# Pairs of tiles only, with queries, keys and values made three units ahead and passed through DRAM

## The chip, the cores and the metric

The kernel runs on one core of a Trainium2 chip, in fp32 throughout. The metric is the device time of one execution in microseconds; the median of three runs counts. The engines are named as in the profile: PE is TensorE (PEld its weight load), DVE is VectorE, ACT is ScalarE, POOL is GpSimd, and SP is the engine whose queue issues nearly all DMAs.

## The reference

Eight images (B = 8) of 512 tokens (S) with 576 features (D) pass through a rotation in a 64-dimensional subspace that depends on a condition, and then through one transformer block whose shifts, scales and gates depend on the same condition. The block has 16 heads of 36 features (H, DH), and its attention is unusual: it runs over the 16 heads *of one token*, not over tokens, so each token has a 16 x 16 matrix of scores.

```python
U, _ = qr(P)                                   # 576 x 64
R = expm(skew(silu(cond) @ W.T + b))           # one 64 x 64 per image
z = einsum('btn,nd->btd', x, U)
x = x + einsum('btd,nd->btn', einsum('btd,bde->bte', z, R) - z, U)
shift_a, scale_a, gate_a, shift_m, scale_m, gate_m = split(silu(c) @ ada_w + ada_b, 6)
h = modulate(layernorm(x), shift_a, scale_a)
q, k, v = (h @ qkv_w + qkv_b).reshape(n, t, 3, H, DH)
attn = softmax(einsum('nthd,ntkd->nthk', q * DH**-0.5, k))
o = einsum('nthk,ntkd->nthd', attn, v).transpose(0, 2, 1, 3).reshape(n, t, d)
x = x + gate_a * (o @ proj_w + proj_b)
h = modulate(layernorm(x), shift_m, scale_m)
x = x + gate_m * (gelu(h @ fc1_w + fc1_b) @ fc2_w + fc2_b)     # hidden width 2304
```

The transpose ahead of the last reshape mixes heads and tokens: row blocks of the projection's input hold many tokens of one head. In each image the 128 rows of one *tile* of the projection come from 8 x 16 places of the attention result. So the attention result goes to DRAM and is read back in the other order.

## The kernel before

A prologue (QR of P, the skew matrices and their exponentials, the modulation) takes some 230 us. Then the work is cut into tiles of 128 tokens, four per image, and these pieces, each a function below, are strung together by hand:

- `rotation(b)` gives six pieces: two of `project_z` (z of half an image, from a transposed copy of x) and four of `rotate` (PE adds the rotation to a tile, VectorE sums it with x, the result is stored to DRAM as `xr` and normalised: `normed`, L130). `feature_major(b, half)` turns the normalised tiles on PE and ScalarE modulates them into `hT`.
- `qkv(b, i)` gives four groups for tile i: ten matrix instructions each (five chunks of D, two passes in the profile's count) into 432 columns of PSUM, and a copy by ScalarE (L803) into a tile `qkv` in SBUF, of which there are three buffers.
- `attention(b, ts)` works on the tiles named in `ts` on VectorE: for each tile four products (L821) and four reductions (L827) of 2304 elements per partition give the scores; then one softmax over all tiles of `ts`, its exponential on ScalarE (L834); then four products and four reductions per tile with the values (L843, L849). The result is stored to DRAM by SP.
- `Projection` loads that result in projection order (`at`) and the rotated x. `turn(t)` transposes a tile (L882) and ScalarE copies it to `aT` (L883); `product(t, n)` multiplies half of the columns (L893), and VectorE gates and adds (L895, L896); `norm(t)` normalises; `turn_normed(cs)` transposes the normalised rows (L911) for the mlp.
- `mlp` runs fc1 (L938) and fc2 for a pair of tiles in nine steps, with weights streamed from DRAM by SP. fc2 takes seven products instead of eight for a pair (sums of blocks: POOL makes those of the activations, L1029 to L1032, and `next_sums`, called nine times early in the kernel, makes those of the weights and stores them as `comb_d`). `mlp_plain` is the ordinary product for a unit of one tile. `aside` slips pieces of the next image's rotation and its `feature_major` between the steps of an mlp.

A *unit* is what one projection and one mlp work on. There are seventeen: the first two tiles of image 0 are units of one tile each, all others are pairs. The main loop takes a unit k, and around its projection places the qkv groups of unit k + 1: three groups ahead of `turn(0)`, one between `turn(0)` and `product(0, 0)`, three ahead of `turn_normed((0, 1))`, one after it. The attention of unit k + 1 is written after the mlp of unit k.

The text gives each engine its instructions in written order only where `manual_schedule` says so: in the kernel before, for POOL until unit 2. Elsewhere a scheduler orders each engine's instructions when the program is built, by priority (earlier written first) and by its estimate of when operands are ready. PE, ScalarE, POOL, VectorE and SP each run their own list in order and wait for each other by semaphores. Buffers in SBUF and banks in PSUM are rings: `ps_mm`, which qkv, rotation and projection share, has two banks, so the third product in a row waits until the first has been read.

## Time and profile before

| | |
|---|---|
| Median of three runs | 2204.76 us (2204.02 to 2207.38) |
| The profiled execution | 2202.1 us, its span 2200.2 us, mean granted clock of TensorE 0.958 |
| Busy: PE, PEld | 2085.2 us (95%), 1562.6 us (71%) |
| Busy: DVE, ACT, POOL | 1795.9 us (82%), 390.0 us (18%), 703.2 us (32%) |
| Moved by DMA | 355.55 MB, mean 162 GB/s; SP's queue holds 16 engines for 54.6% of the span |
| VectorE's longest waits | 134.6 us for the end of an mlp (L1075), 119.8 us for ScalarE's copy of qkv (L821) |

The page first gives the busy time of each engine, then the span in forty slices of 55 us with one digit per slice (9 is 90% or more), among them the clock that TensorE was granted. A line of a group gives the line of the kernel, the engine, output and inputs by their names in the program, shape, count, busy time and mean duration. In a timeline a row is a run of equal instructions: start, duration, engine, line, and in brackets how long the engine was idle just before, with the one that released it. A row of windows gives a stretch: its length, then busy time and count for PE, PEld, DVE, ACT and POOL, the granted clock, the busy share of the sixteen DMA engines and the GB/s that they moved. Rows of DMAs give count, size and the median time from issue to landing.

### The profile page before, as it was taken

What the parts mean: (1) busy time and instruction counts of PE and PEld (TensorE: products, weight loads), DVE (VectorE), ACT (ScalarE), POOL (GpSimd) and SP (SyncE); (2) the same over time, 40 slices, a digit from 0 to 9 for tenths busy, and PEclk for the clock granted to TensorE, in tenths of its full rate; (3) what the DMA queues carried; (4) which work ended last, traced back from release to release, by engine and by line L of the source; (5) the groups of instructions that cost most, each with busy time, mean ns of one, the idle gap of its engine ahead of it and who ended that gap; (6) DMA issues with size and microseconds to landing.
All of it is one profiled execution on the core that took longest, in us unless ns stands there. A gap on an engine that the chain in (4) does not pass through costs nothing.

```text
span 2200.2 us, 26294 instructions
## 1 busy us (share of the span) xinstructions
PE 2085.2 (95%) x9609; PEld 1562.6 (71%) x9609; DVE 1795.9 (82%) x2450; ACT 390.0 (18%) x831; POOL 703.2 (32%) x882
## 2 busy tenths in 40 slices
PE   6896797899999999999999999999999999999998
PEld 3475455667777777868686868777776868686877
DVE  8997498799986979888896979697978889797930
ACT  2232121121021212111111112111211112111110
POOL 2341033113333233424241424243332324142422
PEclk9955698999999999999999999999999999999999
DMA  8201145864757374837384656656573737374764
GB/s 277 86 2 71 45 117 171 285 214 136 218 168 202 118 211 123 234 97 215 113 248 127 170 158 196 162 152 181 158 227 97 221 107 214 106 215 113 210 177 123
DMA packets 214291, 355.55 MB, mean 162 GB/s; under 512 B 82670, under 2 KB 101563, under 8 KB 214164
## 3 DMA queue, kind: packets, MB, share of 16 engines
q1 hardware_dynamic: 214164, 353.88, 54.6%
q8 instruction: 77, 1.26, 0.2%
q14 instruction: 50, 0.41, 0.1%
HBM read 321.43 MB, written 32.39 MB: 161 GB/s over the span
## 4 chain that ended last, share of the span: by engine, by line
PE 57%; DVE 19%; issue 13%; DMA 5%; POOL 3%; ACT 1%; SPq 1%; POOLq 0%; DVEq 0%; ACTq 0%
PE fc L938 24%; PE fc L1044 7%; PE fc L1049 5%; PE qkvp L796 5%; DVE sc L827 4%; DVE pv L843 3%; DVE att L849 3%; PE fc L1046 2%; PE p L1059 2%; DVE qk L821 2%; DMA out<-x 2%; PE zps L731 2%; DMA w<-in_fc_w 1%; PE fc L1001 1%; PE rot L739 1%
## 5 line engine op out<-in xcount | busy, mean ns | idle before, releaser
L938 PE MATMUL fc<-h2T,w 128*128 128x256 f32 (+3 forms) x3060 | 659.9, 369 | 11.4 <-DMA w<-in_fc_w 10.0
L938 PEld LDWEIGHTS fc<-h2T,w 128*128 128x128 f32 (+1 forms) x3060 | 551.9, 192 | 86.1 <-issue 9.8
L796 PE MATMUL qkvp<-wqkv,hT 128*128 128x432 f32 (+1 forms) x1280 | 478.6, 527 | 2.8 <-ACT hT L775 1.4
L821 DVE TENSOR_TENSOR qk<-qkv 128x2304 f32<-128x2304 f32 x128 | 328.9, 2570 | 122.4 <-ACT qkv L803 119.8
L796 PEld LDWEIGHTS qkvp<-wqkv,hT 128*128 128x128 f32 (+1 forms) x1280 | 239.6, 190 | 205.6 <-issue 195.4
L843 DVE TENSOR_TENSOR pv<-sc,qkv 128x2304 f32<-128x2304 f32 x128 | 331.4, 2589 | 3.2
L849 DVE TENSOR_REDUCE att<-pv 128x144 f32<-128x2304 f32 x128 | 326.5, 2551 | 3.2
L827 DVE TENSOR_REDUCE sc<-qk 128x64 f32<-128x2304 f32 x128 | 326.3, 2549 | 2.9
L1029 POOL TENSOR_TENSOR ss<-gt 128x128 f32<-128x128 f32 x135 | 143.4, 1062 | 578.3 <-ACT gt L946 578.3
L946 ACT ACTIVATE gt<-fc 128x512 f32<-128x512 f32 (+1 forms) x153 | 87.5, 572 | 728.7 <-PE fc L938 728.5
L803 ACT COPY qkv<-qkvp 128x432 f32<-128x432 f32 x128 | 66.5, 519 | 542.7 <-PE qkvp L796 542.5
L1049 PEld LDWEIGHTS fc<-wt,ss 128*128 128x128 f32 x1080 | 150.5, 190 | 14.2
L1049 PE MATMUL fc<-wt,ss 128*128 128x144 f32 x1080 | 154.4, 286 | 0.0
L1044 PE MATMUL fc<-wq,gt 128*128 128x288 f32 x540 | 153.0, 405 | 0.0
L140 POOL TENSOR_TENSOR rstd_m<-rstd_m,mhalf 128x1 f32<-128x1 f32 x32 | 19.9, 622 | 371.3 <-DVE rstd_m L139 366.0
L1075 DVE TENSOR_TENSOR u<-u,fc 128x288 f32<-128x288 f32 x15 | 6.8, 454 | 134.6 <-ACT u L1074 134.6
L1044 PEld LDWEIGHTS fc<-wq,gt 128*128 128x128 f32 x540 | 100.8, 189 | 21.3
L893 PE MATMUL pj<-w2q_p,aT 128*128 128x288 f32 x384 | 105.5, 411 | 3.0 <-ACT aT L883 1.4
L954 POOL TENSOR_TENSOR x<-x,mt 128x288 f32<-128x288 f32 x64 | 53.1, 831 | 172.3 <-DVE mt L953 172.3
L1031 POOL TENSOR_TENSOR ss<-gt,ss 128x128 f32<-128x128 f32 x135 | 99.8, 740 | 10.6
L1032 POOL TENSOR_TENSOR s<-gt 128x128 f32<-128x128 f32 x135 | 93.1, 690 | 0.0
L893 PEld LDWEIGHTS pj<-w2q_p,aT 128*128 128x128 f32 x384 | 70.0, 189 | 29.8 <-issue 6.2
(255 smaller groups left out, 2344.4 us busy)
## 6 DMA issues: line engine op xcount, KB each, us to landing
w<-in_fc_w SPq DMA_DIRECT2D x306, 320.0 KB, 3.5
wq<-in_fc_q SPq DMA_DIRECT2D x135, 432.0 KB, 3.4
wt<-comb_d SPq DMA_DIRECT2D x135, 432.0 KB, 4.5
w2q_p<-in_proj_w SPq DMA_DIRECT2D x34, 432.0 KB, 4.9
w<-in_fc_w SPq DMA_DIRECT2D x36, 288.0 KB, 4.6
xT<-in_x_t SPq DMA_DIRECT2D x16, 640.0 KB
w2t_p<-in_proj_w SPq DMA_DIRECT2D x34, 288.0 KB, 4.8
xt<-in_x SPq DMA_DIRECT2D x32, 288.0 KB, 4.5
```

Source lines behind the costliest of these rows:

```text
L796: nc.tensor.matmul(ps, lhsT=hT[0:k, c, i * 128 : (i + 1) * 128], rhs=wqkv[0:k, c, n * N : (n + 1) * N], start=c == 0, stop=c == NK - 1,)
L821: nc.vector.tensor_tensor(pr, q[:, c * HC : (c + 1) * HC].unsqueeze(2).to_broadcast([128, HC, H, DH]), k.unsqueeze(1).to_broadcast([128, H ...
L827: nc.vector.tensor_reduce(sc2[:, t, c * HC : (c + 1) * HC, :], pr, AX.X, ALU.add)
L843: nc.vector.tensor_tensor(pr, sc2[:, t, c * HC : (c + 1) * HC, :].unsqueeze(2).to_broadcast([128, HC, DH, H]), v.unsqueeze(1).to_broadcast ...
L849: nc.vector.tensor_reduce(att[:, c * HC : (c + 1) * HC, :], pr, AX.X, ALU.add)
L893: nc.tensor.matmul(ps, lhsT=aT[0:k, c, :], rhs=w, start=c == 0, stop=c == NK - 1)
L938: nc.tensor.matmul(ps[:, k], lhsT=w1[0:n, c, :], rhs=h2T[0:n, c, 0 : NU * 128], start=c == 0, stop=c == NK - 1,)
L1029: nc.gpsimd.tensor_tensor(ss[:, 0], gt[:, 0, 1], gt[:, 1, 1], ALU.add)
L1031: nc.gpsimd.tensor_tensor(ss[:, 2], gt[:, 1, 0], ss[:, 1], ALU.subtract)
L1032: nc.gpsimd.tensor_tensor(s3s[g], gt[:, 0, 0], gt[:, 0, 1], ALU.subtract)
L1044: nc.tensor.matmul(p[k], lhsT=whole[k][0], rhs=whole[k][1], start=g == 0, stop=stop)
L1049: nc.tensor.matmul(bank[:, side], lhsT=lhs, rhs=rhs[:, n * QUARTER : (n + 1) * QUARTER], start=False, stop=stop, skip_group_check=True,)
```

## The change

All units are pairs, sixteen of them, and `mlp_plain` is gone. A qkv tile is made in six groups of 288 columns. Each group is copied by ScalarE to a small buffer `qs` (two of them) and stored to DRAM (`tok_d`) by a DMA that ScalarE issues; `attention` loads the tile back through SP. Only the first two tiles of image 0 stay in SBUF. The groups are made three units ahead: image 0's four tiles and image 1's four tiles before the first projection, then two tiles in each of units 1 to 10, one tile in each of units 11 to 14, none in unit 15. Rotation and `feature_major` run two images ahead (in the first unit of each image) rather than one.

`attention` becomes a generator of which `ops(n, att)` takes n VectorE operations; its softmax is taken per tile rather than per unit, and the first tile's shares are worked out after the second tile's scores. Up to the norm of the first unit, all of the order is written by hand, for VectorE as for POOL. In the projection of a unit, all groups but the last six come ahead of `turn(0)`, none stands between `turn(0)` and `product(0, 0)`, five come ahead of `turn_normed((0, 1))` and one after it. The bias row of fc2 is no longer kept as a constant (`b2`) but loaded for each image into `gb2`.

```diff
 def qkv(b, i):
-        tok = tiles.tile([128, 3 * D], F32, tag="qkv", name=f"qkv_{b}_{i}", bufs=3)
-        N = 3 * D // 4
+        stay = b == 0 and i < 2
+        if stay:
+            tok = toks[b, i] = tiles.tile([128, 3 * D], F32, tag="qkv", name=f"qkv_{b}_{i}", bufs=3)
...
-            nc.scalar.copy(tok[:, n * N : (n + 1) * N], ps)
-        toks[b, i] = tok
-        return [lambda n=n: group(n) for n in range(4)]
+            if stay:
+                nc.scalar.copy(tok[:, cols], ps)
+            else:
+                qs = tiles.tile([128, HALF], F32, tag="qs", name=f"qs_{b}_{i}_{n}")
+                nc.scalar.copy(qs, ps)
+                nc.scalar.dma_start(out=tok_d[b][i * 128 : (i + 1) * 128, cols], in_=qs)
+        return [lambda n=n: group(n) for n in range(6)]
 def attention(b, ts):
-        own = [toks.pop((b, i)) for i in ts]
+        for i in ts:
+            if (b, i) not in toks:
+                toks[b, i] = tiles.tile([128, 3 * D], F32, tag="qkv", name=f"qkv_{b}_{i}", bufs=3)
+                nc.sync.dma_start(out=toks[b, i], in_=tok_d[b][i * 128 : (i + 1) * 128])
+            own.append(toks.pop((b, i)))
...
+        yield from scores(0)
+        raised(0)
+        yield from scores(1)
+        raised(1)
+        shares(0)
+        yield from values(0)
+        shares(1)
+        yield from values(1)
 
-    units = [(0, (0,)), (0, (1,)), (0, (2, 3))] + [(b, (i, i + 1)) for b in range(1, B) for i in (0, 2)]
+    units = [(b, (i, i + 1)) for b in range(B) for i in (0, 2)]
...
+    held.enter_context(tc.manual_schedule(engines={mybir.EngineType.Pool, mybir.EngineType.DVE}))
+    first[0]()
     feature_major(0, 0)
+    q = qkv(0, 0)
+    now(q[:2])
+    first[2]()
+    now(q[2:4])
+    first[3]()
+    next_sums()
+    now(q[4:])
+    q = qkv(0, 1)
+    att = attention(*units[0])
+    ops(4, att)
+    first[4]()
+    next_sums()
     feature_major(0, 0)
+    ops(2, att)
+    first[5]()
+    now(q)
     next_sums()
     feature_major(0, 1)
+    now(qkv(0, 2))
+    ops(4, att)
     next_sums()
+    second[0]()
+    ops(4, att)
+    second[1]()
     next_sums()
+    ops(2, att)
+    second[2]()
+    now(qkv(0, 3))
+    second[3]()
+    ops(2, att)
+    next_sums()
+    second[4]()
+    ops(2, att)
+    second[5]()
+    next_sums()
+    feature_major(1, 0)
+    now(qkv(1, 0))
+    ops(4, att)
+    next_sums()
+    now(qkv(1, 1))
+    feature_major(1, 1)
+    now(qkv(1, 2))
+    q = qkv(1, 3)
+    now(q[:3])
+    ops(4, att)
+    next_sums()
+    ops(40, att)
+    next_sums()
+    att = attention(*units[1])
+    ops(6, att)
+    ahead = {0: q[3:]}
+    tiles_of = [(unit[0], i) for unit in units[4:] for i in unit[1]]
+    for k in range(1, N - 1):
+        for tile_ in [tiles_of.pop(0) for _ in range(2 if k < 11 else 1)]:
+            ahead.setdefault(k, []).append(tile_)
     for k, (b, ts) in enumerate(units):
         if ts[0] == 0:
             gate_a, gate_m = gate_rows(0, b), gate_rows(1, b)
             gb2 = big.tile([128, D], F32, tag="gb2", name=f"gb2_{b}")
-            nc.gpsimd.tensor_tensor(gb2, gate_m, b2, ALU.mult)
+            nc.sync.dma_start(out=gb2, in_=fc2_b.to_broadcast([128, D]))
+            nc.gpsimd.tensor_tensor(gb2, gb2, gate_m, ALU.mult)
...
+        now(q[:front])
+        pr.turn(0)
+        pr.product(0, 0)
+        pr.turn(1)
+        pr.product(0, 1)
+        pr.norm(0, gb2)
+        pr.product(1, 0)
+        pr.product(1, 1)
+        pr.norm(1, gb2)
         if k == 0:
+            ops(1, att)
+        now(q[front : max(front, len(q) - 1)])
+        pr.turn_normed((0, 1))
+        now(q[max(front, len(q) - 1) :])
         pr.turn_normed((2, 3))
         pr.turn_normed((4,))
+        if k == 0:
+            held.close()
         aside = {}
+        if ts[0] == 0 and b + 2 < B:
+            p = rotation(b + 2)
+            aside = {1: p[0], 2: p[1], 4: p[4], 5: p[5]}
+            aside[3] = lambda two=p[2:4]: now(two)
+            aside |= {7: lambda: feature_major(b + 2, 0), 8: lambda: feature_major(b + 2, 1)}
+        mlp(pr, gate_m, aside)
+        ops(40, att)
+        if k + 2 < N:
+            att = attention(*units[k + 2])
```

## The prediction, made before the changed kernel ran

> **What bounds the kernel now.** I read the page's busy row and slices first, to see which engine is full and where it is not; then the chain's shares; then the timelines of PE (TensorE) where the slices have holes; then windows for clock and DMA.
>
> ```profile
> PE 2085.2 (95%) x9609; PEld 1562.6 (71%) x9609; DVE 1795.9 (82%) x2450; ACT 390.0 (18%) x831; POOL 703.2 (32%) x882
> PE   6896797899999999999999999999999999999998
> DVE  8997498799986979888896979697978889797930
> PEclk9955698999999999999999999999999999999999
> PE 57%; DVE 19%; issue 13%; DMA 5%; POOL 3%; ACT 1%; SPq 1%; POOLq 0%; DVEq 0%; ACTq 0%
> ```
>
> A slice is 55 us. From the tenth on PE is full: what runs there costs its PE time, and only less PE work or fewer holes shorten it. Slices 3 to 8 (110 to 495 us) have holes and a low granted clock. The change begins at about 240 us, so I looked at PE from there to the first pair's mlp.
>
> ```profile
> 268.82 1.33 PE L771 MATMUL htr<-ident,xm 128*128 128x128 f32 x5 [10.92 <-DVE xm L141]
> 279.88 14.78 PE L796 MATMUL qkvp<-wqkv,hT 128*128 128x432 f32 x40 [0.33 <-DVE xt L747]
> 343.06 1.09 PE L911 MATMUL h2tr<-ident,xm 128*128 128x128 f32 x4 [6.30 <-DVE xm L141]
> 361.75 4.58 PE L938 MATMUL fc<-h2T,w 128*128 128x128 f32 x20 [7.96 <-DMA w<-in_fc_w]
> 519.67 2.65 PE L938 MATMUL fc<-h2T,w 128*128 128x256 f32 x11
> ...
> 225.00:245.00 20.00, 18.37 (x56) 12.31 (x56) 4.49 (x14) 4.61 (x15) 1.64 (x13) 0.54 0.28 93
> 365.00:385.00 20.00, 18.52 (x121) 16.43 (x120) 10.51 (x6) 1.67 (x5) 0.00 (x0) 0.97 0.99 275
> sum 300.00, PE 257.90 PEld 174.95 DVE 247.13 ACT 55.99 POOL 68.90; mean PE 17.19 PEld 11.66 DVE 16.48 ACT 3.73 POOL 4.59
> ```
>
> The brackets are the wait before a row and its releaser. Between 225 and 525 us PE is idle 42 us, and partly at half clock besides: VectorE is late twice, and a single-tile mlp waits 8 us for weights while the DMA engines stand at 0.99. Counting every gap over the pace at which matmuls follow each other in full stretches (363 ns for 432 columns, 243 for 288), I find 80 us lost between 225 and 520 us, and under 1 us per unit later.
>
> **A check of the method.** At 519.67 before still owes 15 pair mlps (69.56 us each at pace), 14 pair projections (11.90), 26 qkv tiles (14.51), 6 rotations of an image (11.36): 1655.5 us. 519.7 + 1655.5 = 2175.2; its last matmul ends at 2192.4. So 17.2 us are stalls (8 in the last unit), and 7.8 us of tail make the span. The sum is good to a few us, and the front is where the change can win.
>
> **The change, part by part.**
>
> *Pairs only.* Two single units (43.1 us each) become one pair unit (81.5): 4.7 us less PE work, and the weights are streamed 16 times rather than 17, so the stretch at DMA share 0.99 with its waits (8.0 us, and 4.3 us in fc2) goes.
>
> *qkv in six groups.* A tile is 40 matmuls of 363 ns before, 60 of 243 after: 14.51 against 14.56 us, 1.6 us over 32 tiles. With the rest of the re-cutting PE work after 225 us falls by 3 us only. All else is stalls.
>
> *The front, written by hand.* Queries, keys and values of eight tiles and image 1's rotation now come before the first projection. I followed the written order from the rows above with before's durations: VectorE's attention operation every 2.59 us, a rotated tile 3.1 us, copies 0.4.
> - VectorE's first score at 253.5, as before (image 0's rotation of tiles 2 and 3 keeps its place around it). PE waits for VectorE to free a bank behind the rotations: tile 1 of qkv starts at 273.5 (279.9 before), ends 290.1.
> - VectorE holds behind a rotation that PE has behind qkv of tile 2 (302 to 312), and again (332 to 341). PE waits in turn for VectorE 314 to 321.5 and 343 to 350.5. These are new stalls of the written order; before's scheduler could run attention in between.
> - Image 1's rotation brings two xT and four xt loads and four xr stores onto SP, in windows of DMA share 0.3 to 0.4: no wait. The nine next_sums (POOL, 5.6 us each beside a busy VectorE) put their comb_d stores on SP too; the last three hold SP until 358, 363 and 369, and the store of the first attention tile, behind them, goes at 373: its re-load lands at 384, just in time.
> - qkv of image 1: 353.6 to 384; attention of unit 0 is done at 387, its re-load through DRAM (store 6.9, load 4.2 us by the page) at 398; PE has qkv to do until 410; projection to 420; first fc1 at **429.8**.
>
> The clock: the three PE pauses are 5.6, 7.8 and 7.5 us.
>
> ```profile
> 268.00:272.00 4.00, 1.79 (x6) 1.40 (x7) 3.78 (x3) 1.84 (x5) 0.15 (x1) 0.50 0.27 74
> 272.00:276.00 4.00, 4.00 (x10) 2.73 (x9) 3.96 (x2) 0.00 (x0) 0.00 (x0) 0.50 0.00 0
> 279.00:283.00 4.00, 3.67 (x12) 1.83 (x11) 3.48 (x13) 0.26 (x1) 0.69 (x2) 1.00 0.67 226
> ```
>
> After the 10.92 us pause the granted clock (column after POOL) is 0.50 for two windows with 5.8 us of PE work: 2.9 us lost. The Trainium skill ("TensorE: Matmul & The Clock Gate", "What's actually happening") says that a pause of about 3.4 us halves the clock until some 3.4 us of sustained work: 1.7 us lost. It speaks against a written order that makes three such pauses: 5 us by the page, 9 by the row. I took 2 each, as the shorter pause at 361.75 gives nearly that; the difference is 3 us of the range.
>
> *After 429.8* are owed 16 mlps (1113.0), 15 projections (178.5), 24 qkv tiles (349.4), 6 rotations (68.2), less 1.0 done early: 1708.1. 429.8 + 1708.1 = 2137.9, against 2175.2.
>
> *Steady units lose cover.* In before a group of qkv stands between the turn of the attention result and its product:
>
> ```profile
> 1058.59 0.71 PE L882 MATMUL atr<-ident,at 128*128 128x128 f32 x5
> 1059.14 3.79 PE L796 MATMUL qkvp<-wqkv,hT 128*128 128x432 f32 x10
> 1062.77 1.62 PE L893 MATMUL pj<-w2q_p,aT 128*128 128x288 f32 x6
> ```
>
> After, the product comes at once and waits for ScalarE's copy of aT; unit 0 of before, which had no cover either, waited 0.56, plus the lost pace: 0.73 us, x15 = 11. Before turn_normed five groups (12.1 us) replace three (10.9); xm was late by 0.46 us here, so 0 to 0.6 a unit remain. I take 17 us for 15 units, 8 for the last, 7.8 tail: 2137.9 + 32.8 = **2170.7** span.
>
> *The way through DRAM.* 30 tiles x 0.885 MB, out and back: 53 MB more, some 11 MB less for the dropped unit, on 355.55: about a tenth of the engines' time. Windows of a unit with rotation:
>
> ```profile
> 1080.00:1090.00 10.00, 9.54 (x34) 5.05 (x33) 9.97 (x6) 2.99 (x7) 4.20 (x2) 1.00 0.00 0
> 1120.00:1130.00 10.00, 10.00 (x49) 8.48 (x48) 10.00 (x11) 1.19 (x2) 2.86 (x7) 1.00 0.90 295
> 1140.00:1150.00 10.00, 9.99 (x53) 8.27 (x52) 9.93 (x7) 3.20 (x6) 5.74 (x6) 1.00 1.00 226
> w<-in_fc_w SPq DMA_DIRECT2D x306, 320.0 KB, 3.5
> ```
>
> The stores fall in qkv stretches (share 0.00 to 0.5, last but two columns aside), which have room; the loads come in the mlp, at 0.9 to 1.0, yet no matmul waits there today. The skill ("DMA: Bandwidth & Descriptors", "Issuing engines are not separate DMA queues") says that stores issued from ScalarE run on the same 16 engines as SP's loads and only spare issue time: so they are no free lane. A unit's 3.5 MB at the 295 GB/s seen is 12 us of full engines; the page would let all 12 hurt in a full stretch, the row lets nothing. Bounds: 0 and 12 us per unit; I take 0, since prefetch is a buffer deep everywhere and the mean share is 0.55, and keep 3 us per unit for the range. Below nothing: weights are no longer starved early, already counted.
>
> On SP the loads of a tile wait for its stores and for VectorE to free one of three qkv buffers; behind them stand weights (one every 5 us). The stores land three units earlier, so only VectorE's pace can hold them: 0 to 3 us per unit, taken 0. On ScalarE the qs buffers (two) are free when a store has landed, 3.0 us for xr of twice the size, against 4.85 us of PE between uses of one: hidden, with 1.8 us to spare. gb2's load, its product on POOL and per-tile softmax (some 15 more exps, each with table loads of 1283 ns to and fro) lie beside an 18% busy ScalarE; gelu can come 2 to 3 us late against 4 to 6 us slack: 0, bound 0.7 a unit, what one such slip cost before (L1046 on POOL). VectorE has about 97 us a unit, 107 with a rotation, against PE's 110 and 122; in the last five units PE's 96: bound 0 to 5 us in all.
>
> **Sum.** The profiled execution took 2202.1 us (span 2200.2); the median 2204.76 is 4.6 above the span. 2170.7 + 4.6 = 2175.
>
> **Rivals.**
> - *Slower: SP's queue holds the weights.* A qkv load waiting for VectorE's buffer delays every fc1 and fc2 load behind it; tolerance is one prefetch, about 3.7 us. From 2.3 us lost a unit (34 over 15 units) the gain is gone; at 4 us: 2175 + 60 = 2235. For: shares of 1.00 in the mlp, one queue for all loads, and VectorE 82% busy. Against: VectorE waited 134.6 us for the mlp's end and 119.8 us for qkv, so it has slack. 0.2.
> - *The front is worse.* Each engine waits for the other in written order; if PE's first mlp starts 20 us later, at 450: 2195; at 30: no change. For: five alternating waits of 5 to 10 us. 0.18, a third of it at no change.
> - *Front or steady state better.* Schedules without the 17 us, or a first fc1 at 420: 2157. 0.15.
> - The forecast: 0.47.
>
> **Numbers.** Faster than 2200.3 (0.2% is 4.4 us, about what can be told from no change): 0.47 + 0.15 + 0.11 = 0.73; within: 0.06; slower: 0.21. The range 2155 to 2213 leaves out the far ends of the first and third rival.
>
> **What would show it.** Right: PE's first fc1 of 256 columns near 430, the same 115 us a unit after it, a wait of pj for aT of 0.5 us in each unit, no DMA row under PE's waits in the mlp. Wrong: "fc <- DMA w" or "wt" as large waits in steady units (first rival); htr, rot or qkvp waiting for VectorE by tens of us before 430 (second); VectorE's waits for qkv gone but PE waiting for xm or att instead.

## The result, and the profile after

The changed kernel takes 2266.4 us (median of four runs, 2263.4 to 2267.3) against 2206.1 us for the kernel before, run beside it on the same chip: a ratio of 1.0267, 95% interval 1.0246 to 1.0289. The forecast was 2175, with a range of 2155 to 2213. The kernel is slower by 60 us, and outside the range. The profiled execution has a span of 2265.3 us, 94.6 above the 2170.7 of the sum.

The page of the changed kernel: busy times, the slices of VectorE, the queue of the new stores, and the chain of waits by engine.

```profile
PE 2107.7 (93%) x10087; PEld 1689.8 (75%) x10087; DVE 1820.3 (80%) x2530; ACT 427.2 (19%) x916; POOL 683.9 (30%) x918
DVE  8897668599999999999999997986979536832940
q10 hardware_dynamic: 25920, 26.55, 3.7%
DVE 42%; PE 37%; issue 10%; POOL 4%; DMA 4%; ACT 1%; SPq 0%; ACTq 0%; POOLq 0%; DVEq 0%
```

VectorE's total is hardly changed (1820 against 1796 us), but its slices are. Before, 7s and 8s alternated with 9s to the end. Now sixteen slices in a row (nine to twenty-four, 450 to 1360 us) are at 9, and later ones fall to 5, 3 and 2. In the chain VectorE has 42% and PE 37%, where PE had 57% and VectorE 19%. The average hides this: VectorE is full in the first half, and in the second it has less and less to do.

To place the loss I cut the span at the first transpose of a unit's attention result (`atr`, the start of its projection). The column of forecast is the prediction's own sum, cut at the same places (work of 808.2 and 723.9 us in the two middle rows, plus the 17 us of stalls).

| us | forecast | after | difference |
|---|---|---|---|
| start to unit 1's `atr` | 524.3 | 543.3 | +19 |
| unit 1's to unit 8's (units 1 to 7) | 816 | 859.4 | +43 |
| unit 8's to unit 15's (units 8 to 14) | 733 | 760.0 | +27 |
| unit 15's to the end | 97.3 | 102.7 | +5 |

Windows over units: length, then busy time and count of PE, PEld, DVE, ACT and POOL, granted clock, DMA share and GB/s. First the kernel before: six units in its middle, and of these one with a rotation and one without.

```profile
590.25:1293.93 703.68, 700.33 (x3066) 533.34 (x3064) 584.26 (x504) 120.82 (x221) 243.76 (x283) 1.00 0.59 171
...
823.24:947.21 123.97, 123.49 (x543) 93.71 (x542) 103.31 (x97) 23.48 (x44) 44.31 (x49) 1.00 0.60 178
947.21:1058.59 111.38, 110.91 (x483) 84.58 (x482) 95.37 (x69) 16.96 (x30) 37.31 (x44) 1.00 0.56 158
```

And the changed kernel: units 1 to 7, units 8 to 14, and then unit 3 (without rotation), unit 4 (with one) and a stretch of the length of a late unit.

```profile
543.25:1402.66 859.41, 827.01 (x3835) 677.25 (x3834) 840.31 (x678) 166.72 (x307) 269.68 (x323) 0.99 0.64 193
1402.66:2162.61 759.95, 738.31 (x3476) 610.65 (x3474) 527.79 (x476) 132.73 (x246) 239.65 (x316) 0.99 0.64 195
...
789.55:905.93 116.38, 113.13 (x523) 93.36 (x522) 114.72 (x84) 21.79 (x38) 38.73 (x44) 0.99 0.69 194
905.93:1039.03 133.10, 127.88 (x584) 103.62 (x582) 130.37 (x117) 28.40 (x53) 38.37 (x50) 0.97 0.64 197
1796.00:1894.00 98.00, 96.94 (x462) 81.10 (x462) 37.05 (x45) 14.59 (x28) 28.87 (x45) 1.00 0.62 195
```

Before, VectorE worked 95 us in a unit without rotation and 103 in one with, and PE stood 3.4 us in all six. After, it works 115 and 130 us, where PE's work is 110.6 and 121.9: VectorE sets the pace. In units 1 to 7 it works 840 of 859 us, in the late stretch 37 of 98.

Its groups in units 1 to 7 (count, then busy time and mean ns) say what it works on:

```profile
L859 DVE TENSOR_TENSOR pv<-sc,qkv 128x2304 f32<-128x2304 f32 x72 | 189.5, 2632 | 1.1
L866 DVE TENSOR_REDUCE att<-pv 128x144 f32<-128x2304 f32 x72 | 183.1, 2543 | 1.1
L831 DVE TENSOR_TENSOR qk<-qkv 128x2304 f32<-128x2304 f32 x68 | 177.1, 2604 | 0.8
L838 DVE TENSOR_REDUCE sc<-qk 128x64 f32<-128x2304 f32 x68 | 173.0, 2544 | 0.9
```

That is 280 large operations in seven units, 40 each. A unit's attention is 2 tiles of 16 large operations, 32; before held that number in every unit. In the changed program the list of VectorE has, between the ends of the mlps of successive units, 40, 41, 40, 41, 40, 41, 40 of them, and then 33, 32, 32, 8, 24, 8, 24 and 0. The order is fixed when the program is built. In the text `ops(40, att)` stands behind each mlp and takes the 32 of one unit; that the scheduler moves some of the next unit's forward, because in its estimate data three units ahead are always ready, is my reading and was not traced in the scheduler. What the trace shows is that the brake of before is gone. In the six middle units of before VectorE waited 48 us for qkv; in units 1 to 7 of the changed kernel the same products waited 0.8 us (row L831 above).

```profile
L821 DVE TENSOR_TENSOR qk<-qkv 128x2304 f32<-128x2304 f32 x44 | 112.2, 2551 | 48.8 <-ACT qkv L803 48.0
```

Seventeen extra operations of 2.6 us in two units are 44 us, and the two rows above have 245.1 against before's 198.7.

What this does to PE: the projection of unit 4, on PE and on VectorE (start, duration, and in brackets the wait and its releaser).

```profile
907.56 1.72 PE L921 MATMUL pj<-w2q_p,aT 128*128 128x288 f32 x6 [0.92 <-ACT aT L911]
...
912.10 1.14 PE L921 MATMUL pj<-w2t_p,aT 128*128 128x288 f32 x4
...
915.61 2.36 PE L921 MATMUL pj<-w2q_p,aT 128*128 128x288 f32 x6 [2.37 <-DVE pt L923]
917.76 2.13 PE L921 MATMUL pj<-w2t_p,aT 128*128 128x288 f32 x4
```

```profile
909.95 2.55 DVE L838 TENSOR_REDUCE sc<-qk 128x64 f32<-128x2304 f32 x1
912.53 2.56 DVE L831 TENSOR_TENSOR qk<-qkv 128x2304 f32<-128x2304 f32 x1
915.01 0.45 DVE L923 TENSOR_TENSOR pt<-pj,gate 128x288 f32<-128x288 f32 x1
```

The third product needs a bank that `pt` must read first. `pt` takes 0.45 us, but two attention operations stand ahead of it in VectorE's list, so PE waits 2.37 us. The wait costs more than its length: the four matmuls of the last row take 2.13 us where the same four took 1.14, and the granted clock of that stretch is 0.52.

```profile
917.00:920.00 3.00, 3.00 (x8) 2.13 (x7) 2.39 (x6) 0.00 (x0) 0.00 (x0) 0.52 0.94 308
```

In units 1 to 7 the clock stood at half four times, for 3.4 us each, three of them at a wait for `pt` like this one. That is some 7 of the 43 us. In fs3_lead, the last experiment below, it did not fall in these units.

Four of PE's waits in the whole kernel, in total, times and longest:

```profile
PE pj L921 <- DVE pt L923: 17.6, 11, 3.5
PE qkvp L797 <- DVE xt L746: 12.4, 2, 8.1
PE pj L921 <- ACT aT L911: 9.9, 13, 0.9
PE qkvp L797 <- ACT qs L808: 7.2, 3, 4.4
```

These rows are smaller than the 94.6 us: much of the loss is stretched matmul rows (the busy PE of 827 us in units 1 to 7 has 808 us of work; the halved clock is a part of that) and short gaps. That is why the windows, not the list of waits, carry the reading.

Running ahead has an end: by unit 8 VectorE has used up the lead of three units. Its 353rd large operation, the first for unit 11, needs the tile that unit 8 has only just made. The last of its six stores is issued at 1403.29, SP's load of the tile waits for the stores, and VectorE for the load:

```profile
1403.29 0.33 ACTq L809 DMA_DIRECT2D tok<-qs  x1
1406.64 0.33 SPq L822 DMA_DIRECT2D qkv<-tok  x1
1412.89 2.56 DVE L831 TENSOR_TENSOR qk<-qkv 128x2304 f32<-128x2304 f32 x1 [4.36 <-DMA qkv<-tok]
1415.37 0.82 DVE L923 TENSOR_TENSOR pt<-pj,gate 128x288 f32<-128x288 f32 x2
```

VectorE is idle 4.36 us for a tile's load, for an attention operation that nobody needs for three units yet, while `pt` stands behind it; PE waits 3.48 us for that `pt`. From here the list can only keep up with the tiles as they are made: 32 operations in units 8 to 10, which make two tiles each, and 8 and 24 in turn in units 11 to 14, which make one.

The front, PE first (the forecast had the waits for VectorE at 7.8 and 7.5 us and this first fc1 at 429.8), then ScalarE and its queue:

```profile
323.56 17.71 PE L797 MATMUL qkvp<-wqkv,hT 128*128 128x288 f32 x60 [8.12 <-DVE xt L746]
353.50 0.48 PE L770 MATMUL htr<-ident,xm 128*128 128x128 f32 x1 [7.07 <-DVE xt L746]
380.05 4.38 PE L797 MATMUL qkvp<-wqkv,hT 128*128 128x288 f32 x10 [4.44 <-ACT qs L808]
386.70 11.67 PE L797 MATMUL qkvp<-wqkv,hT 128*128 128x288 f32 x40 [2.27 <-ACT qs L808]
445.87 1.35 PE L966 MATMUL fc<-h2T,w 128*128 128x256 f32 x5
```

```profile
371.14 0.40 ACT L808 COPY qs<-qkvp 128x288 f32<-128x288 f32 x1 [0.99 <-DMA tok<-qs]
375.45 0.33 SPq L1032 DMA_DIRECT2D wt<-comb_d  x1
379.18 0.33 ACTq L809 DMA_DIRECT2D tok<-qs  x1
379.60 0.40 ACT L808 COPY qs<-qkvp 128x288 f32<-128x288 f32 x1 [8.07 <-DMA wt<-comb_d]
386.25 0.40 ACT L808 COPY qs<-qkvp 128x288 f32<-128x288 f32 x1 [6.25 <-DMA tok<-qs]
```

The two waits for VectorE came as worked out. What was not expected is that ScalarE stands 8.07 and 6.25 us ahead of two copies of 0.40 us, and PE, which has two banks, stands behind it. In the first of these waits it is the store that is held, not the copy: the copy into its buffer was done at 371.54, the store goes out at 379.18, just after SP's load of a weight, `wt<-comb_d`, has landed (379.10).

### The profile page after: what moved, and what is told of

It reads as the page before. It is cut to its first block, busy times and chain, and to the rows that moved or that the text cites. A ratio compares the mean times of both kernels' runs of the same rounds, so it can differ in the third digit from the quotient of the medians.

```text
span 2265.3 us, 27889 instructions
## 1 busy us (share of the span) xinstructions
PE 2107.7 (93%) x10087; PEld 1689.8 (75%) x10087; DVE 1820.3 (80%) x2530; ACT 427.2 (19%) x916; POOL 683.9 (30%) x918
## 4 chain that ended last, share of the span: by engine, by line
DVE 42%; PE 37%; issue 10%; POOL 4%; DMA 4%; ACT 1%; SPq 0%; ACTq 0%; POOLq 0%; DVEq 0%
PE fc L966 11%; DVE pv L859 8%; DVE att L866 8%; PE qkvp L797 8%; DVE sc L838 8%; DVE qk L831 7%; PE fc L1037 4%; PE pj L921 3%; PE fc L1042 2%; DMA qkv<-tok 1%; DMA tok<-qs 1%; PE fc L1039 1%; PE p L1052 1%; POOL rstd_a L140 1%; PE dp L270 1%
## 5 line engine op out<-in xcount | busy, mean ns | idle before, releaser
L966 PE MATMUL fc<-h2T,w 128*128 128x256 f32 (+1 forms) x2880 | 654.2, 381 | 5.9 <-ACT h2T L942 5.5
L966 PEld LDWEIGHTS fc<-h2T,w 128*128 128x128 f32 (+1 forms) x2880 | 540.8, 191 | 81.8 <-ACT h2T L942 11.2
L797 PE MATMUL qkvp<-wqkv,hT 128*128 128x288 f32 (+1 forms) x1920 | 488.2, 413 | 24.7 <-DVE xt L746 12.4
L797 PEld LDWEIGHTS qkvp<-wqkv,hT 128*128 128x128 f32 (+1 forms) x1920 | 368.7, 194 | 132.1 <-DVE xt L746 13.9
L831 DVE TENSOR_TENSOR qk<-qkv 128x2304 f32<-128x2304 f32 x128 | 337.5, 2637 | 95.6 <-DMA qkv<-tok 89.5
L1022 POOL TENSOR_TENSOR ss<-gt 128x128 f32<-128x128 f32 x144 | 133.0, 924 | 685.5 <-ACT gt L974 685.5
L866 DVE TENSOR_REDUCE att<-pv 128x144 f32<-128x2304 f32 x128 | 325.7, 2544 | 2.4
L974 ACT ACTIVATE gt<-fc 128x512 f32<-128x512 f32 x144 | 86.0, 597 | 651.1 <-PE fc L966 650.8
L808 ACT COPY qs<-qkvp 128x288 f32<-128x288 f32 x180 | 71.6, 398 | 536.4 <-PE qkvp L797 488.5
L1042 PEld LDWEIGHTS fc<-wt,ss 128*128 128x128 f32 x1152 | 160.7, 190 | 15.0
L1042 PE MATMUL fc<-wt,ss 128*128 128x144 f32 x1152 | 164.7, 286 | 0.0
L1039 PE MATMUL fc<-wq,ss 128*128 128x288 f32 x288 | 94.5, 410 | 6.3 <-POOL ss L1024 6.3
```

Source lines behind the costliest of these rows:

```text
L797: nc.tensor.matmul(ps, lhsT=hT[0:k, c, i * 128 : (i + 1) * 128], rhs=wqkv[0:k, c, cols], start=c == 0, stop=c == NK - 1,)
L831: nc.vector.tensor_tensor(pr, q[:, c * HC : (c + 1) * HC].unsqueeze(2).to_broadcast([128, HC, H, DH]), k.unsqueeze(1).to_broadcast([128, H ...
L866: nc.vector.tensor_reduce(att[:, c * HC : (c + 1) * HC, :], pr, AX.X, ALU.add)
L966: nc.tensor.matmul(ps[:, k], lhsT=w1[0:n, c, :], rhs=h2T[0:n, c, 0 : NU * 128], start=c == 0, stop=c == NK - 1,)
L1022: nc.gpsimd.tensor_tensor(ss[:, 0], gt[:, 0, 1], gt[:, 1, 1], ALU.add)
L1039: nc.tensor.matmul(p[2], lhsT=whole[2][0], rhs=whole[2][1], start=g == 0, stop=stop)
```

## The experiments

Theory: VectorE's list is uneven, attention taken too early in units 1 to 7; beside it, the lost cover of `aT`, and the `qs` waits of the front. Rivals: the way through DRAM (two more passes of every tile over the DMA engines) or the order as such. Times below are medians; each ratio is to the kernel before, run beside it. The table at the end of this section has one profiled execution of each, cut by units.

**e1_even: each unit gets its own attention, in written order.**

```diff
-    att = attention(*units[1])
+    def rest():
+        for k in range(1, N):
+            yield from attention(*units[k], then=units[k + 1] if 2 < k + 1 < N else None)
+    att = rest()
+    def plan(k):      # ahead of turn(0); after norm(1); in steps 0 to 9 of the mlp
+        if k == 0:
+            return 0, 1, [2, 3, 3, 2, 2, 2, 3, 3, 3, 3]
+        if k < 11:
+            if k % 2:
+                return 4, 5, [3, 3, 2, 3, 2, 3, 2, 3, 3, 0]
+            return 4, 5, [3, 3, 2, 2, 2, 2, 3, 3, 3, 1]
+        return 0, 2, [4, 4, 3, 3, 3, 3, 2, 3, 3, 0]
...
+            held.enter_context(tc.manual_schedule(engines={mybir.EngineType.DVE}))
...
-        ops(40, att)
-        if k + 2 < N:
-            att = attention(*units[k + 2])
```

Not shown are a few lines that move the loads of the tiles to where the attention begins with each of them, and the store of an attention tile one step up. e1 thus changes more than the number; e2 below keeps all of this.

> The changed kernel with one thing different after the first unit: VectorE stays in written order, and each unit takes 33 of the attention's large operations (30 in the last units), spread over its projection and its mlp's steps, instead of the 40 or 41 that the scheduler put between two mlps' ends in units 0 to 7. The way through DRAM, the three units ahead, the groups and the front are the same. Theory 'order' (VectorE, given data three units ahead, was loaded past PE's time and served PE late): two units in the steady part take about 235 us instead of 247 to 250, the wait of pj for pt goes, 2266 falls to 2185 to 2205. Rival 'transit' (53 MB more on DMA and ScalarE's issues and copies slow each unit): nothing changes, 2255 to 2270. Rival 'cover' (no group between turn and product): about 1 us a unit of the loss stays, and only that is left after VectorE.

Measured: 2246.0 us (2241.2 to 2251.7), ratio 1.0187 [1.0165, 1.0209]. Units 1 to 7 in windows, and the wait that PE has most of in the steady units:

```profile
548.63:1383.95 835.32, 818.13 (x3836) 675.31 (x3834) 739.98 (x613) 156.26 (x297) 252.35 (x324) 1.00 0.67 197
```

```profile
PE zps L730 <- DVE xt L746: 12.6, 6, 3.1
```

VectorE is down from 840 to 740 us in these units, 105.7 each and so below PE's mean of 115.5 (808.2 over 7); PE's waits for `pt` are all but gone (2.3 us in the whole kernel); units 1 to 7 are 24.1 us shorter. Units 8 to 14 gained nothing (760.8), the last unit lost 2.5, and unit 1 starts 5.4 later, of which 3.3 were there at the first qkv product, ahead of every edit. In units with a rotation the attention operations, now fixed, stand ahead of a rotated tile (`xt`), and PE waits 12.6 us for that (6.2 in the changed kernel). So the mechanism is right and its share too large in the expectation: about 24 of the 43 us.

**e2_early: the same written order, attention early again.** This tells the number of operations from everything else that e1 changed.

```diff
-            return 0, 1, [2, 3, 3, 2, 2, 2, 3, 3, 3, 3]
-        if k < 11:
...
+            return 0, 2, [4, 4, 3, 3, 3, 3, 4, 4, 4, 4]
+        if k < 6:
+            return 5, 6, [3, 3, 3, 2, 2, 3, 2, 3, 3, 3]
...
```

Units 0 to 5 now hold 38 operations each. Unit 0, which the lines above also change, had 28, and its mlp now has 36 instead of 27.

> The same written order as e1_even, but units 1 to 5 take 38 of the attention's large operations each, and later ones fewer. Nothing else differs. Theory 'order': VectorE then has 112 to 113 us of work in a unit without rotation and 122 to 123 with one, against 110.6 and 122 of PE: PE loses 3 to 6 us in each of these units, 15 to 30 us in all against e1_even. Rivals 'transit' and 'cover': the time of e1_even within 4 us.

Measured: 2284.6 us (2280.1 to 2285.4), ratio 1.0357 [1.0341, 1.0372]: 38.6 above e1, more than expected. PE and VectorE in unit 1:

```profile
576.80 3.25 PE L931 MATMUL pj<-w2q_p,aT 128*128 128x288 f32 x6 [23.69 <-DVE pt L933]
```

```profile
576.30 0.45 DVE L933 TENSOR_TENSOR pt<-pj,gate 128x288 f32<-128x288 f32 x1
```

VectorE has fallen behind its list by the end of unit 0's mlp, and unit 1's first `pt` waits for the whole arrears: one wait of 23.69 us, and the granted clock is at half for 27 us (555 to 582). Units 1 to 7 take 880.3 us, 45 more than in e1. Unit 1 has 26.5 of them; units 2 to 5, with the 38 that the expectation was about, have 17.7. Same engine order by hand, same data path, only the count moved: the count is a cause.

**p1_pairs: the kernel before with pairs only.** Units as after, but qkv in four groups of 432 columns, one unit ahead, staying in SBUF. All calls of `next_sums` come ahead of the first product, and image 1's rotation lies in unit 0's mlp.

```diff
-    units = [(0, (0,)), (0, (1,)), (0, (2, 3))] + [(b, (i, i + 1)) for b in range(1, B) for i in (0, 2)]
+    units = [(b, (i, i + 1)) for b in range(B) for i in (0, 2)]
...
-    attention(0, (0,))
-    next_sums()
-    next_sums()
-    now(qkv(0, 2))
+    attention(0, (0, 1))
+    for _ in range(8):
+        next_sums()
```

> The kernel before with one part of the change alone: sixteen pairs; qkv in four groups one unit ahead, in SBUF, as before. By the same sum as in the prediction: VectorE must do both tiles of unit 0 before the first projection, done at about 350, first fc1 at about 395; then 1777 us of PE work, 20 of stalls, 8 of tail: 2200 span, 2205; and some 10 to 15 more if unit 1's attention (83 us, with a rotation 95) is not done within the first mlp (80 us). Expected 2205 to 2220: pairs alone neither gain much nor cost the 60 us. Theory 'pairs are the loss': 2250 or more.

Measured: 2219.4 us (2218.2 to 2222.5), ratio 1.0067 [1.0052, 1.0082].

```profile
350.44 1.33 PE L882 MATMUL atr<-ident,at 128*128 128x128 f32 x5 [38.07 <-DMA at<-att]
```

Dropping the single units saves their PE work and the stretch that was short of weights, but there is then nothing for PE to do during the attention of the first pair: 38.07 us for its first tile and 16.3 for its second. Pairs alone lose; they need the work that the rest of the change puts in front. Its units 1 to 7 take 817.4 us, 9 above the work: this is what before's way of ordering gives.

**p3_cover: one qkv group back between the turn and the product.**

```diff
-        now(q[:front])
+        hold = max(front - 1, 0)
+        now(q[:hold])
         pr.turn(0)
+        now(q[hold:front])
         pr.product(0, 0)
```

> The changed kernel with one group of qkv moved back between turn(0) and product(0, 0) in the units that make two tiles (1 to 10). Theory 'cover': the 0.92 us wait of pj for aT goes in ten units: 9 to 12 us faster than the changed kernel. Theory 'order': in units 1 to 8 VectorE sets the pace and PE waits for pt as much longer: 0 to 4 us faster.

Measured: 2250.4 us (2248.4 to 2253.9), ratio 1.0206 [1.0187, 1.0225]: 16 us less than the changed kernel.

```profile
540.09:1383.39 843.30, 821.65 (x3835) 672.53 (x3834) 831.01 (x677) 164.72 (x305) 262.52 (x323) 1.00 0.67 196
```

PE's waits for `aT` are down from 9.9 to 0.7 us, and units 1 to 7 are 16.1 us shorter. That is more than the cover can be: 0.92 us of wait and the pace lost with it, 1.08 in a unit, is about 11 us in the ten units where the group was moved, and 7.6 in these seven. PE's waits for `pt` did not become less there (11.2 us, and now 12.1 with those ahead of a qkv group), but only one is over 1.3 us, where four were over 1.8, and the clock stood at half for 3.4 us instead of 13.6, which is some 5 us. What is left was not separated. VectorE was idle 12 us instead of 19, and worked 831 us instead of 840 on the same 280 large operations.

**f1_front: room for the copies of qkv in the front.** Three `qs` buffers, and the six pieces of image 1's rotation in two lots, each behind three groups of qkv.

```diff
-    now(qkv(0, 2))
+    q = qkv(0, 2)
+    now(q[:3])
...
     second[1]()
     next_sums()
-    ops(2, att)
     second[2]()
-    now(qkv(0, 3))
-    second[3]()
-    ops(2, att)
+    now(q[3:])
+    ops(4, att)
     next_sums()
+    q = qkv(0, 3)
+    now(q[:3])
+    ops(4, att)
+    next_sums()
+    second[3]()
...
-                qs = tiles.tile([128, HALF], F32, tag="qs", name=f"qs_{b}_{i}_{n}")
+                qs = tiles.tile([128, HALF], F32, tag="qs", name=f"qs_{b}_{i}_{n}", bufs=3)
```

> The changed kernel with another front only: the three qkv groups of tiles 2 and 3 that come last are put behind image 1's rotation pieces, which follow each other directly, so that neither PE nor VectorE waits for the other with attention or qkv in between; and qs has three buffers (the room is taken from a spare buffer of the scores). In the changed kernel PE waited 8.1 and 7.1 us for VectorE there and 7.2 us for qs, and the clock fell. Theory 'front' (these waits add to the steady loss one for one): first fc1 at 425 to 432 instead of 446, 2266 falls to 2246 to 2255. Rival 'VectorE sets the end' (what PE gains early it waits for VectorE later, as VectorE is full until 1320 us): under 8 us faster.

Measured: 2252.9 us (2245.5 to 2254.7), ratio 1.0205 [1.0177, 1.0233]. The first fc1 comes at 433.5 (445.9), unit 1's `atr` at 530.9 (543.3); from there to the end it is like the changed kernel (858.3 and 759.5 us). Of the large waits for `qs` one of 1.5 us is left; a wait of 8.5 us for image 1's last rotated tile is new. The two edits were not separated.

**s1_steady: e1, the cover, and fewer operations ahead of a rotated tile.**

```diff
-            return 0, 1, [2, 3, 3, 2, 2, 2, 3, 3, 3, 3]
+            return 0, 1, [2, 2, 3, 1, 2, 2, 3, 3, 4, 4]
...
-            return 4, 5, [3, 3, 2, 2, 2, 2, 3, 3, 3, 1]
+            return 4, 4, [3, 2, 2, 1, 2, 2, 3, 3, 4, 3]
...
-        now(q[:front])
+        now(q[:hold])
         pr.turn(0)
+        now(q[hold:front])
```

> e1_even with two repairs in the steady part: the group of qkv back between turn(0) and product(0, 0) in units 1 to 10, and in units with a rotation fewer attention operations ahead of the rotated tiles (they are moved to the later steps). Theory: the two add to what e1_even gained: 0.9 us in ten units for the cover, 3 to 5 us in six units for the wait of zps for xt: 2246 falls to 2215 to 2230. Rival: the waits move to other places of the written order, 2240 or more.

Measured: 2225.1 us (2221.8 to 2230.5), ratio 1.009 [1.0068, 1.0112], 21 us under e1. Units 1 to 7 take 826.1, units 8 to 14 752.5; PE's wait for a rotated tile ahead of `zps` is down from 12.6 to 1.8 us. The steady part is now within 18 us of the work in seven units.

**fs_both: f1 and s1 together.** The edits of both, unchanged.

> f1_front and s1_steady together. If front and steady part are independent losses, the gains add: 2195 to 2215, the only version of this plan that could reach the kernel before.

Measured: 2209.6 us (2202.4 to 2216.7, twelve runs), ratio 1.0014 [1.0001, 1.0027]: 15.5 under s1, where f1 had given 13.5. Front and steady state are separate losses.

**t1_twin: s1 with every group stored twice.** The rival that the way through DRAM costs the time: a second, equal store of each group, to a tensor that nobody reads.

```diff
                 nc.scalar.dma_start(out=tok_d[b][i * 128 : (i + 1) * 128, cols], in_=qs)
+                nc.scalar.dma_start(out=twin_d[b][i * 128 : (i + 1) * 128, cols], in_=qs)
```

> s1_steady with every group of qkv stored twice, the second time to a DRAM tensor that nobody reads: ScalarE issues 360 stores instead of 180, and 26.5 MB more are written. Nothing else differs. Rival 'transit' (stores and their issues slow the other engines): as much again as the stores cost today, 10 us or more slower than s1_steady if they made a noticeable part of the 60 us. Theory 'order': within 5 us of s1_steady.

```profile
q10 hardware_dynamic: 51840, 53.11, 7.1%
```

Measured: 2228.9 us (2228.0 to 2233.7), ratio 1.0109 [1.0089, 1.0129]. The queue of the stores moves twice as much, and the kernel takes 3.8 us more than s1, some 3 us in each seven units; the two intervals overlap, so even this is hardly clear of noise. The stores do not carry the loss. The loads of the tiles were not doubled; their only sign in the trace is VectorE's own wait for them.

**fs2_tuned: the attention placed finer.** In the front three operations moved behind the next stretch of qkv; in the units the last three moved by one or two steps; 34 operations in units 2 to 10, fewer late.

```diff
-    ops(4, att)
+    ops(1, att)
...
-    ops(2, att)
+    ops(5, att)
...
-                return 4, 5, [3, 3, 2, 3, 2, 3, 2, 3, 3, 0]
-            return 4, 4, [3, 2, 2, 1, 2, 2, 3, 3, 4, 3]
-        return 0, 2, [4, 4, 3, 3, 3, 3, 2, 3, 3, 0]
+                return n0, 5, [3, 3, 2, 3, 2, 3, 3, 3, 3, 0]
+            return n0, 4, [3, 2, 2, 1, 2, 2, 3, 3, 4, 4]
+        if k < 14:
+            return 0, 2, [4, 3, 3, 4, 3, 3, 3, 3, 0, 0]
+        return 0, 0, [4, 4, 4, 4, 4, 3, 3, 3, 0, 0]
```

> fs_both with three moves of VectorE's written order: three of the attention's operations go behind image 1's last rotated tile (PE waited 8.5 us for it); units 1 to 9 take 34 large operations instead of 33 and units 11 to 13 take 28 instead of 30, none of them in an mlp's last two steps (there PE has only 96 us of work for a unit, less than VectorE's 97, and lost 4 to 6 us each); the last attention ends 8 operations earlier (PE waited 4.4 us for its way through DRAM). If the loss is VectorE's place in each unit, these are worth 8, 12 and 4 us: 2209 falls to 2183 to 2195, faster than the kernel before. If something else holds the plan at the time of before, 2203 or more.

Measured: 2204.1 us (2198.5 to 2209.5, 22 runs) against 2206.5, ratio 0.9988 [0.998, 0.9995]: short of what was expected. The front gave its 10 us (unit 1's `atr` at 512.1 against 522.3), but with one operation more PE's waits for `pt` are back, 5.0 us in fs_both:

```profile
PE pj L931 <- DVE pt L933: 13.2, 6, 5.9
```

Of these, 6.7 us lie in units 3, 5, 7 and 9, where fs_both has none, and 5.9 in unit 11, behind unit 10, which had 33 operations and now has 34, four of them in each of its last two mlp steps. Units 5, 9 and 11 took 114.3, 119.3 and 107.4 us, against 111.6, 112.6 and 101.9 in fs_both.

**fs3_lead: the same with 33 in units without rotation.** 34 stay in those with one, where PE has 11 us more, and 28 in units 11 to 13; the last mlp step of unit 10 holds none.

```diff
-        if k < 11:
-            n0 = 3 if k == 1 else 4
+        if k == 10:
+            return 4, 4, [3, 3, 2, 2, 2, 3, 4, 4, 3, 0]
+        if k < 10:
...
-                return n0, 5, [3, 3, 2, 3, 2, 3, 3, 3, 3, 0]
+                return 3 if k == 1 else 4, 5, [3, 3, 2, 3, 2, 3, 2, 3, 3, 0]
```

> fs2_tuned with VectorE's share of each unit cut to what fs_both and fs2_tuned each did without a wait: 34 large operations in units with a rotation, 33 in the others (34 there made PE wait 1 to 3 us for pt, and more behind it), 28 in units 11 to 13, and none in the last steps of units 10 and 14, behind which the next projection comes at once (unit 11 lost 9 us there). Theory 'VectorE's place': 15 to 18 us of fs2_tuned's waits go, 2204 falls to 2185 to 2193. If 2200 or more, what is left is not VectorE's share per unit.

Measured: 2194.4 us (2191.6 to 2195.5, five runs) against 2204.9 for the kernel before (nine runs), ratio 0.995 [0.9932, 0.9968]. This version beats both kernels, by 0.5% and 3%; 2185 to 2193 was expected. Its page and its units 1 to 7:

```profile
PE 2084.5 (95%) x10087; PEld 1679.5 (77%) x10087; DVE 1855.5 (85%) x2530; ACT 423.9 (19%) x914; POOL 658.7 (30%) x918
DVE  8898469789988998899988998899889989897930
...
515.79:1340.09 824.30, 815.44 (x3835) 673.87 (x3834) 750.27 (x619) 157.54 (x298) 247.76 (x326) 1.00 0.68 200
```

VectorE's slices alternate again, 8s and 9s from the eighth to nearly the end. It moves the same data the same way, with 35 us more VectorE time than the changed kernel has, and is 72 us shorter.

Against fs2 its gain lies late: unit 9 takes 112.0 us instead of 119.3, unit 11 99.9 instead of 107.4, the last unit 3.3 less. Units 1 to 7 are the same (824.3 and 825.6), and so nearly are PE's waits for `pt` in units 3, 5, 7 and 9 (5.8 us after 6.7), though these have 33 operations again. So one operation less in such a unit may be what helped unit 9, but it did not help the units before; unit 11 gained where the end of unit 10 was emptied.

All profiled executions, cut by units (us):

| | first qkv product | unit 1's `atr` | units 1 to 7 | units 8 to 14 | last unit | span |
|---|---|---|---|---|---|---|
| forecast | 240.3 | 524.3 | 816 | 733 | 97.3 | 2170.7 |
| after | 242.7 | 543.3 | 859.4 | 760.0 | 102.7 | 2265.3 |
| e1_even | 246.0 | 548.6 | 835.3 | 760.8 | 105.2 | 2249.9 |
| e2_early | 246.1 | 545.6 | 880.3 | 752.1 | 105.0 | 2282.9 |
| p3_cover | 244.5 | 540.1 | 843.3 | 761.6 | 104.9 | 2249.9 |
| f1_front | 245.1 | 530.9 | 858.3 | 759.5 | 103.0 | 2251.6 |
| s1_steady | 240.3 | 540.0 | 826.1 | 752.5 | 104.6 | 2223.2 |
| t1_twin | 240.6 | 541.9 | 829.1 | 755.5 | 105.5 | 2232.0 |
| fs_both | 240.3 | 522.3 | 824.7 | 751.8 | 104.4 | 2203.2 |
| fs2_tuned | 240.4 | 512.1 | 825.6 | 759.0 | 106.3 | 2203.0 |
| fs3_lead | 245.7 | 515.8 | 824.3 | 747.7 | 103.0 | 2190.7 |

The first qkv product starts ahead of every edit (the forecast's is that of the kernel before). It lies between 240.3 and 246.1 us, so a difference of less than 6 us in unit 1's `atr` says nothing by itself; from the first qkv product to unit 1's `atr` the changed kernel takes 300.5 us, f1 285.8, fs3 270.1.

## Why the prediction was wrong, point by point

**The step that failed: "VectorE has about 97 us a unit, 107 with a rotation, against PE's 110 and 122 … bound 0 to 5 us in all."** The figures come from a total shared out over the units, and for a kernel that shares its attention out they are near: before has 95 and 103, e1 105.7 in the mean of units 1 to 7. But the changed program does not share it out. Its list has 40 or 41 large operations a unit and not 32, hence 115 and 130 us against PE's 110.6 and 121.9. I had written that before's scheduler "could run attention in between", and did not carry it on to the units after the hand-written front: with data three units ahead, what held VectorE back in before, that attention could not start until its qkv was made (119.8 us of VectorE's waits), is gone until unit 8. The order is fixed when the program is built, so the 40 could have been counted before any run: eight or nine operations of 2.6 us would have turned 97 into 118 to 120 us, over PE's 110.6: a loss, where I saw slack. What it cost: e1 took 24 of the 43 us in units 1 to 7 back, and e2, which put the early operations in again, lost 45 there, 26.5 of them behind the overfull unit 0. The rest is the next point, with what goes with it.

**"Steady units lose cover": right in kind, too small.** It was 0.73 us a unit, taken from unit 0 of before, where ScalarE had nothing else. The wait alone is 0.92, with the pace 1.08: ScalarE first makes the copy to `qs` (0.40) and issues the store (0.33). Over the thirteen units that show it, that adds 5 us. Giving the cover back (p3) was worth 16, of which some 5 came by the clock.

**"The front, written by hand": the waits for VectorE right, a wait for ScalarE missed.** The two waits named at 7.8 and 7.5 us measured 8.1 and 7.1. The term that failed is "qs buffers … hidden, with 1.8 us to spare". It allowed for one thing only, a store's landing, at the 3.0 us of before's `xr` stores. ScalarE's first stop is another: the store of 379.18 first waits 7.6 us for the semaphore that is to tell of its own landing, because SP's load `wt<-comb_d` uses the same one ahead of it, and SP could issue that load only at 375.45, behind the last store of `next_sums`. (The 1148 DMAs in this trace tell of their landing by eight semaphores, and both queues use all eight.) The second stop is a landing: that store, issued at 379.18, has landed at 386.17, after 7.0 us, with the DMA engines full (a share of 1.02 from 380 to 386.2). PE lost 4.44, 2.27 and 1.56 us to all this, and the granted clock was 0.75 in the 12 us from 378. Image 1's first two tiles ended at 398.4 (the end of the 40 matmuls at 386.70) instead of 384: 3.1 us of that were there when they began (356.7 against 353.6; 2.4 of them at the first qkv product, 242.7 against before's 240.3), 8.3 are these waits, and 3 are left for the clock; and the first fc1 came at 445.9 instead of 429.8. f1 took 12.4 us of that back. "The front is worse", a rival, thus came near (first fc1 at 450 in it), but it explains 19 of 95 us.

**"The way through DRAM … I take 0": right, as far as tried.** Storing everything twice took 3.8 us more, hardly clear of noise. PE has no wait for weights in any mlp of a pair among its listed waits, so "SP's queue holds the weights", the rival on the slower side, cost nothing. But SP's queue was held, and not as I had it: "only VectorE's pace can hold them" was wrong, SP also waited for stores.

```profile
SPq L822 <- DMA tok<-qs: 132.2, 18, 18.8
```

97 us of this lie from unit 8 on, where the lead is gone. The longest, 18.8 us to 1685.6, fell into a stretch in which PE made qkv (from 1666.2), and the next weight was issued at 1687.4, when PE had freed its buffer. So the tolerance of 3.7 us that the rival took does not hold there. The sign that I named was the one to look for; the loss came by another road, from VectorE. The last named sign, "VectorE's waits for qkv gone but PE waiting for xm or att instead", was near: in units 1 to 7 they are gone, and PE waited for `pt`. In the whole kernel they are 89.5 us, all from unit 8 on.

**"Pairs only": no gain on its own.** The 4.7 us and the 8 us at the weights are not a saving by themselves (p1: 0.7% slower); the filled front turns them into one.

**The late units and the end.** 8 us of stalls for the last unit were taken, 97.3 in all; it is 102.7 to 106.3 in every kernel of this plan, and 98.1 in p1. The traces show one wait there that before and p1 do not have: the projection stands for the last attention, in the changed kernel and f1 2.6 us for VectorE and then 1.3 for the way through DRAM, in p3 1.8 and 4.0, in the others 3.9 to 5.4 for that way. Units 8 to 10, in which the lead is used up, take 365 us against 340 of work (fs3 350); that is most of the loss of units 8 to 14. Units 11 to 14 take 98.4 to 99.3 against 96.0 of work; 1.25 us in each is the first fc1's wait for ScalarE's copy of `h2T`, which before does not have, and the rest stays open. fs3 is at its span 20 us over the forecast, 8 in units 1 to 7, 15 in units 8 to 14, 6 in the last, with a front 8.5 better (14 from the first qkv product on). The structure could do most of what I forecast for it; the order in the changed program could not.

One reading of the slices was off by one: slices 3 to 8 end at 440 us, not 495. Nothing hangs on it.

## What to carry to other kernels

When a change frees an engine from waiting for its data, count its instructions between two fixed points of each stage in the built program, and set that count times its duration against the engine that bounds; a total divided by the number of stages says nothing about a list that is fixed beforehand. An engine that runs ahead makes its short, urgent instructions late, and when the lead is used up holds them behind work that nobody needs yet: give it a quota per stage, smaller in a stage that is shorter. And see in the slices whether a busy share is even: 80% can be 98% in seven units and 38% in a late one.

## What the runs showed of the hardware

- A store of ScalarE's queue waited for a load of SP's queue with which it shares no data. What ties them is the program's semaphore for the landing: the load that used it before had to land first (379.10), and the store went out at 379.18. The stores ahead of it were not slow: the packets of the one issued at 370.18 had all started by 372.
- A wait of PE of 2.37 us was followed by a granted clock of one half for 3.4 us (unit 4 of the changed kernel, above). In units 1 to 7 the three waits for `pt` of 2.33 to 2.51 us all were, and one of 1.81 us (unit 2) was not.
- The products of VectorE took longer in its full stretch: 2632 ns (`pv`) and 2604 (`qk`) in units 1 to 7 of the changed kernel, 2581 and 2570 in those of e1, 2576 and 2551 in the middle of before. The reductions did not change (2544 to 2552). It is not all products that are longer. Of the 140, 65 ran with no operation of POOL beside them and took 2546 ns in the mean, none over 2560; 20 took over 2650, and beside every one of them POOL was at work. Over the 20 that is some 9 us. No run tried the cause.
